# Attention in a four-layer kernel: the spread maximum and the value sums take turns in two PSUM banks

## The chip, the cores and the metric

The kernel runs on one core of a Trainium2 chip. The metric is the device time of one execution in microseconds (us); the figure for a kernel is the median of its timed runs. Engines are named as in the profile: PE (TensorE, matrix products), PEld (its weight loads, which run beside PE), DVE (VectorE), ACT (ScalarE), POOL (GpSimd), SP (SyncE, which issues transfers).

## The reference

Four layers work on `x` of shape (2, 128, 64, 64) in 32-bit floats. Layers 0 and 3 are state-space scans and aren't touched. Layers 1 and 2 are attention over the L = 64·64 = 4096 places of an image, with 128 channels, for each of the two images:

```python
# layer 1 (k and v from an upsampled context; a 3x3 convolution follows)
attn = softmax(einsum('bcn,bcm->bnm', q, k), axis=-1)
out  = einsum('bcm,bnm->bcn', v, attn).reshape(B, C, H, W)
return sr_feat + gamma[0] * conv2d(out, Wp, bp, 1)
# layer 2
attn = softmax(einsum('bci,bcj->bij', q, k), axis=-1)
out  = _conv1x1(einsum('bij,bcj->bci', attn, v), Wo, bo)
return out + x
```

So for each query place n: 4096 scores, their maximum, the exponentials of score minus maximum, their sum, and the sum of values weighted by them.

## The kernel before, in words

**Jobs, groups, units, slots.** Layers 1 and 2 have two images each: four jobs. A job has NG = 16 groups of NQ = 256 queries; there are 64 groups in all. A group goes over the 4096 keys in UPG = 16 units of 256 keys. The order is written out by hand (`tc.manual_schedule()`): one loop over slots, in which every engine gets its instructions in the order of the calls and works through them in that order. A slot issues the score of unit u of one group, the `larger` of the unit before, the softmax steps of the group before it, and two value products; `u` below is slot modulo 16. An odd u or "odd slot" refers to that number.

**The steps of one group, with its first slot called 0.**
- `score(u)`, slots 0 to 15: two products (L961) put the scores of 256 keys by 256 queries into one PSUM bank `s`. ACT copies them to SBUF (`sc`, L966).
- `larger(u)`, one slot later: DVE keeps an elementwise maximum `mx` of 128x2x256 (L973). For u = 0 there is no instruction; for u = 1 both operands are taken at once.
- `turn`, slot 17 (u = 1): PE transposes `mx` in four pieces (L979). `top`, slot 18: DVE reduces them to the maximum `m` of each query (L983), and ACT makes two diagonal matrices `dg` from it (L986). `spread`, slot 19 (u = 3): PE multiplies ones with `dg`, so that bank `pm` holds each query's maximum on all 128 partitions (L992).
- `prob(w)`, w = 0 to 7, slots 21, 23, ..., 35 (odd u): DVE subtracts `pm` from four score tiles in place (L996). `expo(w)` one slot later: ACT (L999). `total(w)` then adds up on POOL (L1004), `total_end` closes it (L1008, L1009).
- `value(u)`, slots 24 to 39: two products (L1016) add onto bank `av`. The group thus has its values for u = 8 to 15 and then 0 to 7 of the slot number.
- `den`, slot 40 (u = 8): PE sums over partitions (L1021), DVE takes the reciprocal (L1023). `finish`, slot 42 (u = 10): DVE multiplies reciprocal and `av` (L1029 or L1036).
- `query`, at u = 10: the next group's queries (L943), with an ACT bias (L945).

Two records on PE stand for each product call in 32-bit floats, one for a transpose. So a score unit or a value unit is four records.

**What is between.** `put` hangs other steps onto slots, after the calls above: key and value pieces of the next job, and after each image of layer 1 the convolution, for groups 1 to 8 of the two jobs that follow: `columns` at u = 10 (four DVE instructions, L1065 to L1068), and `product` at u = 11, 12, 13 and 14 (six PE records each, L1076).

**PSUM.** The eight banks are: `misc` 1, `s` 4 (used in turn by scores, queries, `turn` and `den`), `pm` 1, `av` 2. A bank holds 512 numbers on each partition; `pm` and `av` fill half of one.

Of the kernel before, what the change touches and what calls it, by code (L numbers as in the profile page):

```python
# [8 lines left out]
AF = mybir.ActivationFunctionType  # L9
ALU = mybir.AluOpType  # L10
AX = mybir.AxisListType
PSUM = bass.MemoryType.PSUM

P = 128
# [37 lines left out]
def _bc(ap, axis, shape):  # L52
    return ap.unsqueeze(axis).to_broadcast(shape)
# [3 lines left out]
def conv_seq_kernel(ctx: ExitStack, tc: tile.TileContext, a: dict, out: bass.AP):  # L57
    nc = tc.nc
    mm = nc.tensor.matmul
    act = nc.scalar.activation  # L60
# [3 lines left out]
    def gt(shape, name, pool=None, **kw):  # L64
        return (pool or gp).tile(shape, F32, tag=name, name=name, **kw)
# [14 lines left out]
    ident = cst[:, _CI : _CI + 128]  # L80
    ones = gt([P, P], "ones")
# [16 lines left out]
    with ExitStack() as c0:  # L98
# [153 lines left out]
        def turn(j):  # L252

            nc.scalar.copy(
                xnt[:, 3 + j * T : 3 + (j + 1) * T].rearrange("p (w h) -> p w h", h=H),
                xn[:, 3 : L + 3].rearrange("p (h w) -> p w h", w=W)[:, 8 * j : 8 * j + 8, :],
            )

        class Chunk:
# [110 lines left out]
            def spread(self, what, i):  # L370

                src = (self.ddu if what == "dus" else self.ddt)[i]
                t = wt(what, 2, (P, 4, T))
                for n in range(4):
                    nc.sync.dma_start(t[32 * n : 32 * n + 32], src.rearrange("(k d) t -> d k t", d=32))
                for q in range(2):
                    getattr(self, what)[2 * i + q] = t[:, 2 * q : 2 * q + 2, :]
# [118 lines left out]
        with tc.manual_schedule():  # L496
# [114 lines left out]
            for k, c in enumerate(chunks):  # L611
# [3 lines left out]
                def at(u):  # L615
                    return (c, u) if 0 <= u < 16 else ((old, u + 16) if u < 0 else (new, u - 16))

                A, V, M, G = {}, {}, {}, {}  # L620
                if old is not None:
# [5 lines left out]
                if new is not None:  # L627
# [6 lines left out]
                    M[5], V[6] = lambda: new.pt(1), lambda: new.dt_(1)  # L634
                    G[7], G[8] = lambda: new.dtu_(0), lambda: new.dtu_(1)
                    if not new.rev:
# [23 lines left out]
                if k in turns:  # L660
                    A[11] = (lambda: turn(turns[k]),)

                for s in range(16):
# [7 lines left out]
                    if cp is not None:  # L671
                        cp.s_hc(up)
                    if s in G:
                        G[s]()

# [136 lines left out]
    with ExitStack() as c1:  # L812
        NQ = 256
        NG = L // NQ
        NU = L // 512
        UPG = 2 * NU
# [13 lines left out]
        def bank(tag, shape=(P, T), bufs=1):  # L830
            return ps.tile(list(shape), F32, tag=tag, name=tag, bufs=bufs)
# [4 lines left out]
        def small(tag, shape, bufs=None):  # L836
            return sm.tile(list(shape), F32, tag=tag, name=tag, bufs=bufs)
# [23 lines left out]
        class Job:  # L861
# [77 lines left out]


            def query(self, g):
                pq = bank("s", bufs=4)
                mm(pq[:, :NQ], lhsT=self.wqT, rhs=x[:, self.b, g * NQ : (g + 1) * NQ], start=True, stop=True)  # L943
                q = small("q", (P, NQ))
                act(q, pq[:, :NQ], AF.Identity, bias=self.bq)  # L945
                return q

        class Group:
# [20 lines left out]
            def larger(self, u):  # L969
                if u == 0:  # L970
                    self.mx = small("mx", (P, 2, NQ))
                else:
                    nc.vector.tensor_max(self.mx, self.s[0][:, 0:2, :] if u == 1 else self.mx, self.p[u])  # L973

            def turn(self):
                self.pt = bank("s", (P, 2, 2, P), bufs=4)
                for h in range(2):
                    for o in range(2):
                        nc.tensor.transpose(self.pt[:, h, o, :], self.mx[:, o, h * P : (h + 1) * P], ident)  # L979

            def top(self):
                m = small("m", (P, 2))
                nc.vector.tensor_reduce(m, self.pt, AX.XY, ALU.max)  # L983
                self.dg = small("dg", (P, 2, P))
                for h in range(2):
                    act(self.dg[:, h, :], ident, AF.Copy, scale=m[:, h : h + 1])  # L986

            def spread(self):

                self.pm = bank("pm", (P, NQ))  # L990
                for h in range(2):
                    mm(self.pm[:, h * P : (h + 1) * P], lhsT=ones, rhs=self.dg[:, h, :], start=True, stop=True)  # L992

            def prob(self, w):
                s = self.s[w]
                nc.vector.tensor_sub(s, s, _bc(self.pm[:, :], 1, [P, 4, NQ]))  # L996

            def expo(self, w):
                act(self.s[w], self.s[w], AF.Exp)  # L999
# [9 lines left out]
                self.adds.tensor_add(a_[:, 0, :], a_[:, 0, :], a_[:, 1, :])  # L1009

            def value(self, u):
                if u == 0:
                    self.av = bank("av", (P, NQ), bufs=2)
                for o in range(2):
                    m = 2 * u + o
                    mm(self.av, lhsT=self.job.v[m // 8][:, m % 8, :], rhs=self.s[u // 2][:, m % 4, :],  # L1016
                       start=(m == 0), stop=(m == 31))

            def den(self):
                self.pd = bank("s", (P, NQ), bufs=4)  # L1020
                mm(self.pd, lhsT=ones, rhs=self.sum[:, 0, :], start=True, stop=True)  # L1021
                self.rb = small("rb", (P, NQ))
                nc.vector.reciprocal(self.rb, self.pd)  # L1023
# [82 lines left out]
        def put(slot, *steps):  # L1106
            for i, f in enumerate(steps):
                todo.setdefault(slot + i, []).append(f)

        def piece(slot, j, what, qd, later=0):  # L1110

            steps = []

            def first():
                steps.extend(getattr(j, what)(qd))
                steps[0]()

            n = 2 if j.layer == 2 else 7 if what == "value_piece" else 5
            put(slot, first, *[lambda i=i: steps[i]() for i in range(1, min(n, 5))])
            put(slot + 5 + later, *[lambda i=i: steps[i]() for i in range(5, n)])  # L1120
# [69 lines left out]
        with tc.manual_schedule():  # L1190
            k0, k1 = (jobs[0].key_piece(qd) for qd in range(2))
            k0[0]()
            nc.sync.dma_start(m1[:, 0:128], a["m1"][:, 0:128])
            k1[0]()
            nc.sync.dma_start(m1[:, 128:], a["m1"][:, 128:])
            nc.sync.dma_start(m2, a["m2"])
            for f in k0[1:]:
                f()
            groups[0].q = jobs[0].query(0)
            for f in k1[1:]:  # L1200
                f()
            piece(0, jobs[0], "key_piece", 2)
            piece(4, jobs[0], "key_piece", 3)
            for qd in range(4):
                piece(8 + 5 * qd, jobs[0], "value_piece", qd, 2)
            put(50, second, thirds, second_bias)
            put(60, middle_taps)

            def at(slot):
                n, u = divmod(slot, UPG)  # L1210
                return (groups[n], u) if slot >= 0 and n < len(groups) else (None, 0)

            for slot in range((len(groups) + 2) * UPG):
                u = slot % UPG
                G = at(slot)[0]
                if G is not None:
                    G.score(u)
                    nxt = at(slot + UPG)[0]
                    if u == 10 and nxt is not None:
                        nxt.q = nxt.job.query(nxt.g)  # L1220
                G, d = at(slot - 1)
                if G is not None:
                    G.larger(d)
                G = at(slot - UPG)[0]
                if G is not None:
                    if u == 1:
                        G.turn()
                    if u == 2:
                        G.top()
                    if u == 3:  # L1230
                        G.spread()
                G, d = at(slot - UPG - 5)
                if G is not None and d % 2 == 0:
                    G.prob(d // 2)
                G, d = at(slot - UPG - 6)
                if G is not None and d % 2 == 0:
                    G.expo(d // 2)
                G, d = at(slot - UPG - 8)
                if G is not None:
                    G.value(d)  # L1240
                G, d = at(slot - UPG - 7)
                if G is not None and d % 2 == 0 and d:
                    G.total(d // 2)
                G, d = at(slot - 2 * UPG)
                if G is not None:
                    if d == 6:
                        G.total_end()
                    if d == 8:
                        G.den()
                    if d == 10:  # L1250
                        G.finish()
                for f in todo.get(slot, []):
                    f()
# [4 lines left out]
    with ExitStack() as c3:  # L1258
# [252 lines left out]
        V, G = nc.vector, nc.gpsimd  # L1511
# [263 lines left out]
```

## Time and profile before

| | |
|---|---|
| median of three runs | 6548.74 us (6545.72 to 6561.89) |
| the profiled execution, from its first to its last instruction | 6564.3 us |
| the attention stage in it | about 3470 to 5595 us |
| busy in the whole span | PE 89%, DVE 86%, POOL 83%, ACT 68% |
| one score or value unit on PE, start to start | 0.86 to 0.87 us |
| one `prob` on DVE, mean | 1212 ns |
| one `larger` on DVE, mean | 680 ns |
| one reciprocal on DVE, median | 1757 ns |

The page gives the span of the profiled execution and no time around it. It is 15.6 us, or 0.24%, above the median of the timed runs and 2.4 us above the longest of them. In a line of groups the columns are: line, engine and operation, output and inputs, shapes, count, busy time and mean ns of one, idle time just before and what ended it. In a line of the timeline: start in us, length in us, engine, line, operation, output and inputs; in brackets the idle time before it and what ended it. The length of a PE record ends with its result, later than the start of the next record.

### The profile page before, as it was taken

Reading aid. Unit: us, or ns where it says so; the run is one execution under the profiler, and the core shown is the slowest. Engines: PE = TensorE matmul, PEld = TensorE weight load, DVE = VectorE, ACT = ScalarE, POOL = GpSimd, SP = SyncE. Lnnn points to the kernel's source line nnn. Section 1 sums busy time; section 2 is a strip of 40 time slices with the busy share of each in tenths; the row PEclk is TensorE's granted clock in tenths of the full one; section 3 lists DMA queues with packets and bytes.
Section 4 is the critical chain, followed back from the end, with each engine's and each line's share of the span. In section 5 each row is a group of like instructions: output and inputs, shape, how many; then the busy total and the mean of one; then the engine's idle time right before and its main releaser. Section 6 shows DMA issues by size and latency. Waiting matters only on the chain. (4 is left out here: it accounts for less than half of the span.)

```text
span 6564.3 us, 66618 instructions
## 1 busy us (share of the span) xinstructions
PE 5817.9 (89%) x20014; PEld 2781.5 (42%) x20014; DVE 5628.5 (86%) x4540; ACT 4487.8 (68%) x7771; POOL 5420.7 (83%) x2543
## 2 busy tenths in 40 slices
PE   8888888888888888888888999999999999898888
PEld 2222222222222222222226888888888788222221
DVE  7999999999999999999997766666666766899997
ACT  7887778877788777887766665555556565555453
POOL 6999999999999999999995666655666566788886
PEclk7888777877788777887779999999999999889897
DMA  6566656566666666556650000000000000877775
GB/s 181 145 156 161 161 142 146 146 150 148 152 155 151 153 152 152 146 146 152 151 137 19 2 4 3 1 1 1 1 1 1 2 6 7 205 173 179 181 180 121
DMA packets 400476, 700.36 MB, mean 107 GB/s; under 512 B 74089, under 2 KB 76658, under 8 KB 399730
## 3 DMA queue, kind: packets, MB, share of 16 engines
q1 hardware_dynamic: 399232, 694.33, 43.3%
q8 instruction: 157, 2.57, 0.2%
q14 instruction: 205, 1.68, 0.1%
q10 hardware_dynamic: 882, 1.78, 0.1%
HBM read 584.53 MB, written 111.28 MB: 106 GB/s over the span
## 5 line engine op out<-in xcount | busy, mean ns | idle before, releaser
L383 POOL TENSOR_TENSOR dbu<-dus,bs 128x1024 f32<-128x1024 f32 x1024 | 2448.1, 2440 | 116.9 <-DVE h L427 98.8
L427 DVE TENSOR_TENSOR_SCAN h<-da,hst,dbu 128x1024 f32<-128x1024 f32 x896 | 2090.9, 2340 | 86.1 <-ACT dbu L411 80.7
L396 ACT ACTIVATE da<-dts,aneg 128x512 f32<-128x512 f32 (+1 forms) x2048 | 1410.1, 689 | 357.1 <-DVE h L427 318.9
L1004 POOL TENSOR_TENSOR sum<-sum,sc 128x1024 f32<-128x1024 f32 x378 | 898.1, 2376 | 504.1 <-ACT sc L999 500.4
L966 ACT COPY sc<-s 128x512 f32<-128x512 f32 x1024 | 596.9, 585 | 767.8 <-PE s L961 639.2
L961 PE MATMUL s<-q,k 128*128 128x256 f32 x4096 | 1053.8, 380 | 9.7 <-ACT lo L919 5.5
L1016 PE MATMUL av<-sc,v 128*128 128x256 f32 x4096 | 1051.2, 380 | 9.1 <-ACT sc L999 9.1
L450 PE MATMUL y<-hc,cst 128*32 128x512 f32 x4096 | 880.4, 753 | 200.2 <-DVE hc L439 186.6
L973 DVE TENSOR_TENSOR mx<-mx,s 128x512 f32<-128x512 f32 x896 | 609.3, 680 | 452.5 <-ACT sc L966 449.2
L439 DVE TENSOR_TENSOR hc<-h,pc 128x1024 f32<-128x1024 f32 x704 | 841.9, 1196 | 9.5 <-PE y L450 7.4
L961 PEld LDWEIGHTS s<-q,k 128*128 128x128 f32 x4096 | 777.0, 191 | 126.9 <-issue 8.8
L1016 PEld LDWEIGHTS av<-sc,v 128*128 128x128 f32 x4096 | 768.0, 190 | 112.9 <-ACT sc L999 14.1
L437 POOL TENSOR_TENSOR hc<-h,cs 128x1024 f32<-128x1024 f32 x320 | 770.0, 2406 | 1.2 <-issue 1.2
L416 PE MATMUL pc<-xd,sel 16*128 16x512 f32 x1024 | 707.0, 780 | 0.2
L1407 POOL TENSOR_TENSOR A<-A,D 128x1024 f32<-128x1024 f32 x224 | 526.9, 2370 | 138.8 <-DVE D L1412 102.1
L996 DVE TENSOR_TENSOR sc<-sc,pm 128x1024 f32<-128x1024 f32 x512 | 620.5, 1212 | 0.9 <-PE pm L992 0.9
L999 ACT ACTIVATE sc<-sc 128x1024 f32<-128x1024 f32 x512 | 541.8, 1058 | 41.2 <-DVE sc L996 41.0
L450 PEld LDWEIGHTS y<-hc,cst 128*32 128x32 f32 x4096 | 125.9, 120 | 858.3 <-DVE hc L439 427.6
L340 PE MATMUL misc<-xd,w_dt 9*128 9x512 f32 x504 | 364.6, 810 | 128.1 <-ACT x L479 68.5
L411 ACT ACTIVATE dbu<-hst,dbu,df 128x1 f32<-128x1 f32 x896 | 337.6, 377 | 65.3 <-POOL dbu L383 42.7
L1424 PE MATMUL q<-xs,room 32*128 32x512 f32 x840 | 291.1, 706 | 63.1 <-DVE A L1430 62.1
L416 PEld LDWEIGHTS pc<-xd,sel 16*128 16x128 f32 x1024 | 181.6, 218 | 350.2 <-issue 296.8
(315 smaller groups left out, 7792.9 us busy)
## 6 DMA issues: line engine op xcount, KB each, us to landing
dts<-ddt SPq DMA_DIRECT2D x512, 256.0 KB, 5.4
dus<-ddu SPq DMA_DIRECT2D x512, 256.0 KB, 5.1
D<-rows SPq DMA_DIRECT2D x448, 256.0 KB, 6.0
bs<-rows SPq DMA_DIRECT2D x1024, 64.0 KB, 4.9
cs<-rows SPq DMA_DIRECT2D x1024, 64.0 KB, 3.2
ddt<-dt SPq DMA_DIRECT2D x128, 256.0 KB, 2.0
ddu<-dtu SPq DMA_DIRECT2D x128, 256.0 KB, 4.0
dtr<-ddt SPq DMA_DIRECT2D x448, 64.0 KB, 2.0
```

Source lines behind the costliest of these rows:

```text
L383: nc.gpsimd.tensor_mul(t, self.dus[q], _bc(self.bs[g], 1, [P, 2, T]))
L396: act(t[:, i, sl], self.dts[q][:, i, sl], AF.Exp, scale=an[:, g, 2 * q + i : 2 * q + i + 1])
L416: mm(t, lhsT=sel[32:48, 4 * g : 4 * g + 4, :].rearrange("p n d -> p (n d)"), rhs=self.xd[32:48, :], start=True, stop=True)
L427: nc.vector.tensor_tensor_scan(ho, ai, bi, init, ALU.mult, ALU.add)
L437: nc.gpsimd.tensor_mul(t, self.h[u], _bc(self.cs[gq(u)[0]], 1, [P, 2, T]))
L439: nc.vector.tensor_mul(t, self.h[u], _bc(self.pc[u // 2], 1, [P, 2, T]))
L450: mm(self.y[q // 2][r : r + 32, :], lhsT=sum4, rhs=self.hc[u][:, i, :], start=False, stop=(u % 8 >= 6), skip_group_check=True)
L961: mm(p[:, o, :], lhsT=j.k[m // 8][:, m % 8 * P : m % 8 * P + P], rhs=self.q, start=True, stop=True)
L973: nc.vector.tensor_max(self.mx, self.s[0][:, 0:2, :] if u == 1 else self.mx, self.p[u])
L996: nc.vector.tensor_sub(s, s, _bc(self.pm[:, :], 1, [P, 4, NQ]))
L1004: self.adds.tensor_add(self.sum, self.s[0] if w == 1 else self.sum, self.s[w])
L1016: mm(self.av, lhsT=self.job.v[m // 8][:, m % 8, :], rhs=self.s[u // 2][:, m % 4, :], start=(m == 0), stop=(m == 31))
```

## The change

Three things are different. First, `spread` no longer multiplies ones with a diagonal: it transposes a column of `m`, broadcast to 128 columns, in two pieces; the two ACT instructions for `dg` are gone. Second, DVE joins the two halves of `mx` to one (`join`, called right after the last `larger` of a group), so that `turn` has two transposes in place of four and `top` reduces half as many numbers. Third, the banks: `pm` and `av` of a group are now the halves of one bank `pmav`, of which there are two, taken in turn by the groups; `query`, `turn` and `den` share one bank `aux`; the four `s` banks are left to the scores (and to two late steps of the next layer).

```diff
             def query(self, g):
-                pq = bank("s", bufs=4)
+                pq = bank("aux")
...
+            def join(self):
+                nc.vector.tensor_max(self.mx[:, 0, :], self.mx[:, 0, :], self.mx[:, 1, :])
+
             def turn(self):
-                self.pt = bank("s", (P, 2, 2, P), bufs=4)
+                self.pt = bank("aux", (P, 2, P))
                 for h in range(2):
-                    for o in range(2):
-                        nc.tensor.transpose(self.pt[:, h, o, :], self.mx[:, o, h * P : (h + 1) * P], ident)
+                    nc.tensor.transpose(self.pt[:, h, :], self.mx[:, 0, h * P : (h + 1) * P], ident)
 
             def top(self):
-                m = small("m", (P, 2))
-                nc.vector.tensor_reduce(m, self.pt, AX.XY, ALU.max)
-                self.dg = small("dg", (P, 2, P))
+                self.m = small("m", (P, 2))
+                nc.vector.tensor_reduce(self.m, self.pt, AX.X, ALU.max)
+
+            def spread(self):
+
+                t = bank("pmav", (P, 2, NQ), bufs=2)
+                self.pm, self.av = t[:, 0, :], t[:, 1, :]
                 for h in range(2):
-                    act(self.dg[:, h, :], ident, AF.Copy, scale=m[:, h : h + 1])
-
-            def spread(self):
-
-                self.pm = bank("pm", (P, NQ))
-                for h in range(2):
-                    mm(self.pm[:, h * P : (h + 1) * P], lhsT=ones, rhs=self.dg[:, h, :], start=True, stop=True)
+                    nc.tensor.transpose(self.pm[:, h * P : (h + 1) * P],
+                                        self.m[:, h : h + 1].to_broadcast([P, P]), ident)
 
             def prob(self, w):
                 s = self.s[w]
-                nc.vector.tensor_sub(s, s, _bc(self.pm[:, :], 1, [P, 4, NQ]))
+                nc.vector.tensor_sub(s, s, _bc(self.pm, 1, [P, 4, NQ]))
...
             def value(self, u):
-                if u == 0:
-                    self.av = bank("av", (P, NQ), bufs=2)
...
             def den(self):
-                self.pd = bank("s", (P, NQ), bufs=4)
+                self.pd = bank("aux", (P, NQ))
...
                     G.larger(d)
+                    if d == UPG - 1:
+                        G.join()
```

## The prediction

> **What bounds the kernel now.** I read the page's slices first (the attention stage has PE at nine tenths, DVE and POOL at six), then the groups of the page, the waits of PE in the stage, and one group on the timeline. The groups:
>
> ```profile
> L966 ACT COPY sc<-s 128x512 f32<-128x512 f32 x1024 | 596.9, 585 | 767.8 <-PE s L961 639.2
> L961 PE MATMUL s<-q,k 128*128 128x256 f32 x4096 | 1053.8, 380 | 9.7 <-ACT lo L919 5.5
> L1016 PE MATMUL av<-sc,v 128*128 128x256 f32 x4096 | 1051.2, 380 | 9.1 <-ACT sc L999 9.1
> L973 DVE TENSOR_TENSOR mx<-mx,s 128x512 f32<-128x512 f32 x896 | 609.3, 680 | 452.5 <-ACT sc L966 449.2
> L996 DVE TENSOR_TENSOR sc<-sc,pm 128x1024 f32<-128x1024 f32 x512 | 620.5, 1212 | 0.9 <-PE pm L992 0.9
> ```
>
> Scores and values alone keep PE busy for 2105 of the stage's some 2125 us (3470 to 5595), and PE hardly waits for either. ACT and DVE wait for PE. So PE sets the pace, and whatever makes it wait is paid in full. Its waits between 3500 and 5560 us:
>
> ```profile
> PE pm L992 <- DVE sc L996: 49.8, 52, 1.6
> PE pm L992 <- ACT sc L966: 7.7, 8, 1.1
> ```
>
> That is the one regular wait: the next group's `spread` wants the single `pm` bank while the last `prob` still reads it. On the timeline (group period 30.56 us, from one reciprocal's start, 5338.55, to the next, 5369.11):
>
> ```profile
> 5338.55 1.76 DVE L1023 RECIPROCAL rb<-s 128x256 f32<-128x256 f32 x1 [1.66 <-PE s L1021]
> 5340.22 0.63 DVE L973 TENSOR_TENSOR mx<-mx,s 128x512 f32<-128x512 f32 x1
> 5340.77 1.21 DVE L996 TENSOR_TENSOR sc<-sc,pm 128x1024 f32<-128x1024 f32 x1
> ...
> 5345.69 1.03 PE L961 MATMUL s<-q,k 128*128 128x256 f32 x4
> 5345.70 0.69 DVE L973 TENSOR_TENSOR mx<-mx,s 128x512 f32<-128x512 f32 x1 [0.47 <-ACT sc L966]
> 5346.30 1.21 DVE L996 TENSOR_TENSOR sc<-sc,pm 128x1024 f32<-128x1024 f32 x1
> 5346.55 1.03 PE L1016 MATMUL av<-sc,v 128*128 128x256 f32 x4
> 5346.75 0.59 ACT L966 COPY sc<-s 128x512 f32<-128x512 f32 x1
> 5347.41 1.03 PE L961 MATMUL s<-q,k 128*128 128x256 f32 x4
> ...
> 5357.10 1.21 DVE L996 TENSOR_TENSOR sc<-sc,pm 128x1024 f32<-128x1024 f32 x1
> 5358.46 0.68 PE L992 MATMUL pm<-dg,ones 128*128 128x128 f32 x4 [0.95 <-DVE sc L996]
> ```
>
> Units follow each other every 0.865 us. A value unit (5346.55) runs while DVE subtracts `pm` (5346.30): today they use different banks. And a bank is never used by two engines at once here: the `larger` of most units needs nothing from ACT, yet 449 us of DVE's idle time before L973 end with ACT's copy of the same scores. Two engines that only read one bank are kept apart.
>
> **Bank sharing, the part that decides.** With `pm` and `av` halves of one bank, the same must hold between `prob` on DVE and `value` on PE. The built order of the changed program says so: the values at u = 9, 11, 13, 15, 1 and 3 carry a wait on DVE, and the `prob` ahead of them (the group's third to eighth) comes after PE's values of the slot before, by its own wait or by an earlier one on its engine. At u = 5 and 7 `prob` reads the other bank. Queued behind the waiting value on PE are all later scores, so ACT and DVE starve too.
>
> *The usual odd slot (u = 13, 15).* S is the start of the score in the slot before. Its records end at S+1.03, ACT copies from S+1.08 to 1.67, `larger` starts at 1.70, `prob` 0.60 later (5345.70 to 5346.30) at 2.30, ends at 3.51, and PE starts 0.15 after (5358.31 to 5358.46), at S+3.66. Unhindered the value would start after three units, S+2.595. Stall: 1.07 us. The lower bound is that `larger` is early and only the value before counts (it ends at S+1.90, `prob` from 1.95 to 3.16): 0.72.
>
> *u = 1*: no `larger`, and two transposes (0.22) lie between: 1.95+1.21+0.15 less 2.595 and 0.22, 0.50. *u = 3*: 1.07 less the new `spread` (0.22), 0.85. *u = 11*: the query (0.43) lies between score and value, so `prob` follows the value's end at S+2.38 and PE starts at 3.74, not 3.025: 0.71.
>
> *u = 9*: `den` and the reciprocal come first on DVE. From V, the start of the value at u = 8: `den` is over at V+1.46, the reciprocal starts at 1.50, `larger` 1.67 later, `prob` 0.55 after that (5338.55, 5340.22, 5340.77), PE at V+1.50+1.67+0.55+1.21+0.15 = V+5.08; unhindered at V+2.16. Stall: 2.92 us. Today that delay vanishes in the four score banks.
>
> *Groups with a convolution (16 of 64)*: `columns` at u = 10 takes 1.44+0.86+0.50+0.50 = 3.29 us on DVE, ahead of the `prob` at u = 11. From the value at u = 9: 0.60+0.33+3.29+0.60+1.21 = 6.1 us, against 3.89 unhindered: 2.2. The products at u = 12 and 14 (six records, 1.29) cover the 1.07 at u = 13 and 15.
>
> Sums: 2.92+0.71+2·1.07+0.50+0.85 = 7.12 us in 48 groups, 2.92+2.2+0.50+0.85 = 6.47 in 16: 342+104 = **445 us**. With the lower bounds (0.72 at 13 and 15, 0.50 at 3) it is 6.07 and 6.1, 390. Upwards, a stalled value must also show its first weight load, 0.19 us by its row: 64·6·0.19 = 73 more.
>
> The Trainium skill, "PSUM — Partial Sum Buffer" (section "PSUM bank collisions raise a hardware error"), speaks against this change: it says that two engines collide in a bank even at different addresses, and asks for semaphores by bank. By that rule all six waits are needed; had it been by address, the sum would have only the gains below.
>
> **What the change takes away.** The wait for `pm` goes, 49.8+7.7 and 1.2 for ACT's `dg`: 59 us. `turn` halves (four records in 0.44, start to start, so 0.22), and `spread` falls from four records in 0.52 to two, taken at a transpose's 0.11 each (upper bound: nothing gained if broadcasting costs what is saved): 0.22+0.30 in 64 groups, 33 us. Together **92 us**. The two `dg` (0.69 us of ACT per group), the shorter `top` and the added `join` (nearest row, a 128x256 operation, 0.41 us) cost or bring nothing: DVE idles about 2.1 us before each even-slot `larger` of the new rhythm, and the join stands over 2 us ahead of `turn`. Were that cover gone, the join would cost 64·0.41 = 26. `query` in `aux` waits for the reciprocal, which at u = 9 is over by V+3.3, before the query's turn. No DMA changes.
>
> **The clock.** One long PE gap in the stage, 4011.48 to 4014.23 us (2.75 us, waiting for POOL), is followed by this (the seventh column is the granted clock):
>
> ```profile
> 4012.00:4014.00 2.00, 0.00 (x0) 0.00 (x0) 0.01 (x1) 0.00 (x0) 2.00 (x2) 1.00 0.00 0
> 4014.00:4015.00 1.00, 0.77 (x5) 0.77 (x6) 0.00 (x0) 0.08 (x1) 0.17 (x1) 0.89 0.00 0
> 4015.00:4018.00 3.00, 3.00 (x8) 2.36 (x8) 0.00 (x0) 1.84 (x3) 0.00 (x0) 0.50 0.00 0
> 4018.00:4019.00 1.00, 1.00 (x7) 0.82 (x6) 0.23 (x1) 0.21 (x1) 0.10 (x1) 0.90 0.00 0
> ```
>
> Half clock for 3.4 us, 1.7 us lost. Gaps of 1.69 us (before 5575.65) and 1.43 had no such sequel. The stall at u = 9 is 2.92 less the 0.17 by which a result outlasts its record: a gap of 2.75 too. Bounds: never (0) and in all groups (64·1.7 = 109). The single row of that length lost the clock, the shorter ones didn't; I take 4 in 10, **44 us**. The Trainium skill, "TensorE: Matmul & The Clock Gate" (section "What's actually happening"), wants an idle window of about 3.4 us for the drop; by that the term would be 0, and the row above is against it.
>
> **Sum.** 445 − 92 + 44 = 397 on a span of 6564.3, 6961. The span lies 15.6 over the median of the timed runs: 6945 us.
>
> **Rivals.**
> - *Clock lost in every group* (0.12): all 109 and the weight loads' 73: 445−92+182 = 535, 7084 us. For it the row above; against it 5570 to 5590 us, where PE is busy for 72 and 80% of ten microseconds each at full clock.
> - *Only the reciprocal bites* (0.08): if DVE gets ahead so that the other five `prob`s end before PE is ready: 64·2.92 − 92 = 95, 6644 us. Against it: `prob` alone takes 1.21 us and only one unit of 0.865 lies between the values that bracket it.
> - *Faster* (0.08): the waits fall on values that DVE has long served, and the gains stand: 6549 − 92 = 6457 us, PE almost without a gap. This decides as soon as `prob`, from the preceding value's end to PE's restart (0.05+1.21+0.15), fits into what PE has between; it has 0.865 and needs 1.4. A fourth of this chance is a tie.
> - *My forecast* (0.72), own range 6846 (lower bounds, no clock lost) to 7045.
>
> **Numbers.** The range, 6800 to 7070, takes the forecast's case whole and part of the first rival; the other two and the rest are left out. A measurement of this kernel tells about 0.3% from no change. Faster 0.06, same 0.02, slower 0.92.
>
> **What would show it.** Right: after the change PE has new idle time, ended by DVE's subtraction, before the values (now L1015): some 7 us per group, 384 waits or fewer where products cover them, the longest about 2.9 us at u = 9; DVE's subtraction waits for PE's value; the wait before `spread` is gone; the period of a group without convolution is near 36 to 37 us in place of 30.6. Wrong: values that start every 1.73 us throughout; stalls at u = 9 only; or a granted clock near 0.5 through whole groups, which no term here holds.

## The result, and the profile after

The changed kernel takes 6938.25 us (median of 4 runs, 6935.52 to 6948.86) against 6550.14 us for the kernel before, measured beside it. The ratio is 1.0595 (95% interval 1.058 to 1.061): slower by 6%. The profiled execution spans 6936.3 us, 372 us more than that of before. The attention stage, from the first score's start to the last value's end, grew from 2118.1 to 2510.1 us; the other layers, which the change doesn't touch, happened to be 20 us shorter.

The page's groups after the change, in the same columns as before:

```profile
L1015 PE MATMUL pmav<-sc,v 128*128 128x256 f32 x4096 | 1125.8, 399 | 343.6 <-DVE sc L997 341.6
L966 ACT COPY sc<-s 128x512 f32<-128x512 f32 x1024 | 598.7, 586 | 1187.1 <-PE s L961 1109.8
L961 PE MATMUL s<-q,k 128*128 128x256 f32 x4096 | 1087.4, 390 | 6.8 <-ACT lo L919 5.5
L997 DVE TENSOR_TENSOR sc<-sc,pmav 128x1024 f32<-128x1024 f32 x512 | 621.6, 1214 | 85.7 <-PE pmav L1015 85.4
```

The value products (L1016 before, L1015 now) had 9.1 us of idle time ahead of them and now have 343.6, ended by DVE's subtraction. The subtraction itself takes as long as before (1214 ns), but now waits 85.4 us for PE's values. The scores, products of the same shape (L961), hardly wait (6.8 us). ACT's idle time before its copies has grown by 419 us, and the part of it that PE's scores end by 471: it starves behind PE. So a loop has appeared: DVE waits for a value, the next value waits for DVE. The waits of PE between 3500 and 5940 us, the three most costly of five, show that the former first line, `spread` waiting for `pm`, is gone:

```profile
PE pmav L1015 <- DVE sc L997: 329.1, 333, 4.2
PE misc L896 <- POOL up L936: 2.8, 1, 2.8
PE pmav L1015 <- ACT sc L966: 1.8, 1, 1.8
```

One group on the timeline, without convolution, some of its lines. The first is the restart at u = 9 (one period, 38.0 us, later it comes again in the last line), the second the restart at u = 13, an odd slot of the usual kind, the third and fourth the subtraction and the restart at u = 15:

```profile
5661.17 1.16 PE L1015 MATMUL pmav<-sc,v 128*128 128x256 f32 x4 [2.66 <-DVE sc L997]
...
5672.10 1.13 PE L1015 MATMUL pmav<-sc,v 128*128 128x256 f32 x4 [0.86 <-DVE sc L997]
...
5675.43 1.21 DVE L997 TENSOR_TENSOR sc<-sc,pmav 128x1024 f32<-128x1024 f32 x1
5676.70 1.13 PE L1015 MATMUL pmav<-sc,v 128*128 128x256 f32 x4 [0.88 <-DVE sc L997]
...
5694.19 1.03 PE L1015 MATMUL pmav<-sc,v 128*128 128x256 f32 x4
5695.05 0.59 PE L1020 MATMUL aux<-sum,ones 128*128 128x256 f32 x2
5695.68 1.76 DVE L1022 RECIPROCAL rb<-aux 128x256 f32<-128x256 f32 x1 [1.66 <-PE aux L1020]
5697.90 1.21 DVE L997 TENSOR_TENSOR sc<-sc,pmav 128x1024 f32<-128x1024 f32 x1
5699.16 1.17 PE L1015 MATMUL pmav<-sc,v 128*128 128x256 f32 x3 [2.66 <-DVE sc L997]
```

The subtraction that began at 5675.43 ends at 5676.64; PE restarts at 5676.70. At u = 9 the chain is longer: sum over partitions, reciprocal, `larger`, subtraction, value. The idle time in brackets is counted from the end of PE's last result; measured from one record's start to the next, less the 0.216 us that a record takes, the stall is 2.82 us at u = 9 and 1.02 at u = 13 and 15.

The clock around that first restart (start:end; the seventh column is the granted clock):

```profile
5657.00:5661.00 4.00, 1.51 (x8) 0.98 (x6) 3.31 (x3) 1.57 (x3) 2.35 (x1) 1.00 0.00 0
5661.00:5662.00 1.00, 0.83 (x4) 0.76 (x5) 1.00 (x3) 0.00 (x0) 0.00 (x0) 1.00 0.00 0
5662.00:5665.00 3.00, 3.00 (x9) 2.41 (x8) 0.30 (x2) 0.66 (x2) 0.00 (x0) 0.52 0.00 0
```

Work is there again, but PE runs at half clock for three microseconds. In the trace's clock record the stage has 47 such stretches, 184 us in all; before the change it had one of 3.4 us.

### The profile page after: what moved, and what is told of

The parts are those of the page before. It is cut to its first block, busy times and chain, and to the rows that moved or that the text cites. A ratio compares the mean times of both kernels' runs of the same rounds, so it can differ in the third digit from the quotient of the medians.

```text
span 6936.3 us, 66161 instructions
## 1 busy us (share of the span) xinstructions
PE 5908.6 (85%) x19758; PEld 2791.1 (40%) x19758; DVE 5672.8 (82%) x4604; ACT 4462.3 (64%) x7643; POOL 5410.2 (78%) x2543
## 3 DMA queue, kind: packets, MB, share of 16 engines
q14 instruction: 206, 1.69, 0.1%
## 4 chain that ended last, share of the span: by engine, by line
PE 34%; DVE 17%; POOL 12%; DMA 12%; ACT 11%; issue 10%; SPq 3%; ACTq 0%; POOLq 0%; DVEq 0%
PE pmav L1015 12%; PE s L961 9%; POOL dbu L383 7%; DVE sc L997 6%; DVE h L427 4%; POOL hc L437 3%; DMA dus<-ddu 3%; ACT da L396 3%; PE misc L281 3%; DMA D<-rows 2%; DVE hc L439 2%; DMA cs<-rows 2%; ACT sc L966 2%; DVE D L1413 2%; DMA dts<-ddt 2%
## 5 line engine op out<-in xcount | busy, mean ns | idle before, releaser
L1015 PE MATMUL pmav<-sc,v 128*128 128x256 f32 x4096 | 1125.8, 399 | 343.6 <-DVE sc L997 341.6
L961 PE MATMUL s<-q,k 128*128 128x256 f32 x4096 | 1087.4, 390 | 6.8 <-ACT lo L919 5.5
L1015 PEld LDWEIGHTS pmav<-sc,v 128*128 128x128 f32 x4096 | 774.3, 196 | 560.9 <-DVE sc L997 461.5
L961 PEld LDWEIGHTS s<-q,k 128*128 128x128 f32 x4096 | 801.3, 196 | 133.4 <-issue 9.8
L997 DVE TENSOR_TENSOR sc<-sc,pmav 128x1024 f32<-128x1024 f32 x512 | 621.6, 1214 | 85.7 <-PE pmav L1015 85.4
```

The source lines that it names most:

```text
L961: mm(p[:, o, :], lhsT=j.k[m // 8][:, m % 8 * P : m % 8 * P + P], rhs=self.q, start=True, stop=True)
L997: nc.vector.tensor_sub(s, s, _bc(self.pm, 1, [P, 4, NQ]))
```

## The experiments

The theory: the whole loss comes from `pm` and `av` lying in one bank; the join, the fewer transposes and the broadcast column are a small gain by themselves; and the stall at u = 9 also costs the clock. The rivals: the new operations cost time, or the bank `aux` does; the clock drops for another reason.

**1. The new operations alone** (join, two transposes, broadcast `spread`), with the banks of before:

```diff
-                self.pt = bank("aux", (P, 2, P))
+                self.pt = bank("s", (P, 2, P), bufs=4)
...
-                t = bank("pmav", (P, 2, NQ), bufs=2)
-                self.pm, self.av = t[:, 0, :], t[:, 1, :]
+                self.pm = bank("pm", (P, NQ))
```

The diff is against the changed kernel; `query` and `den` go back to `s`, and `av` to two banks of its own.

> The kernel before with its banks, and only the join, the two transposes and the broadcast spread added. Theory (all the loss is the shared bank): PE sheds four records less per group at turn and spread, 33 us, and the wait for pm at spread stays at about 0.9 us: 6517 us, no wait of a value on DVE, one half-clock interval as before. Rival (join or broadcast column cost time): a value or turn waits for DVE, or the two spread transposes take as long as the four records they replace: 6550 or more.

Measured: 6532.35 us, ratio 0.9953 to before (0.9938 to 0.9969). Its wait of `spread` stands as before:

```profile
PE pm L991 <- DVE sc L996: 52.7, 61, 1.5
PE av L1016 <- ACT sc L999: 9.1, 12, 1.4
...
PE s L981 <- DVE mx L976: 7.3, 6, 2.1
```

So the operations bring about 31 us by the ratio (0.47% of 6556.58, the median of before beside it; the interval is 20 to 41) and 29.6 by the stage (2088.5 us), and none of the loss is theirs. The join is not quite free: `turn` waited for it six times, 7.3 us in all, where before it had waited once, 0.9 us.

**2. The banks alone**, with the diagonal, the four transposes and no join:

```diff
-                self.pm = bank("pm", (P, NQ))
+                t = bank("pmav", (P, 2, NQ), bufs=2)
+                self.pm, self.av = t[:, 0, :], t[:, 1, :]
...
-                pq = bank("s", bufs=4)
+                pq = bank("aux")
```

> The kernel before with only the banks changed: pm and av of a group in one bank, query, turn and den in one. Theory: the waits of values on DVE are there as in the changed kernel. PE has about 0.5 us more work per group at u = 1 and 3, but there DVE sets PE's restart, so that work is covered: about 6940 us, at most 33 more. Rival (the join and the broadcast bring the loss): 6550.

Measured: 6941.32 us, ratio 1.0578 (1.0558 to 1.0598), the same as the changed kernel within the intervals, and a stage of 2509.7 us against 2510.1, with the same kind of wait:

```profile
PE pmav L1015 <- DVE sc L997: 312.5, 278, 4.2
```

The banks are the whole loss. The additional PE work (28 us in the stage, by the pitches of its records) is lost in it, because it lies where DVE sets PE's restart.

**3. Own banks, everything else as changed.** To make room, the scores have three banks in place of four:

```diff
-                t = bank("pmav", (P, 2, NQ), bufs=2)
-                self.pm, self.av = t[:, 0, :], t[:, 1, :]
+                self.pm = bank("pm", (P, NQ))[:, :]
...
+                if u == 0:
+                    self.av = bank("av", (P, NQ), bufs=2)
```

> The changed kernel with pm and av in banks of their own again (one for pm, two for av, and therefore three score banks instead of four); join, broadcast spread and the shared aux bank stay. Theory (the loss is the sharing of pm and av): no value waits for DVE any more, the wait of spread for pm is back with about 0.9 us per group, no clock drops: about 6525 us, and up to some 40 more if three score banks don't cover the reciprocal. Rival (aux or the added join and transposes bring part of the loss): 6600 or more with values waiting for DVE.

Measured: 6528.96 us, ratio 0.9944 (0.9924 to 0.9964), as experiment 1. The stage takes 2088.6 us, 0.1 more than in experiment 1. No value waits for DVE, the old wait of `spread` is back, and one half-clock stretch is left:

```profile
PE pm L991 <- DVE sc L996: 52.7, 61, 1.5
PE s L961 <- DVE mx L973: 8.7, 9, 2.4
...
PE aux L981 <- DVE mx L976: 5.5, 6, 1.9
```

The second and third lines are what the three score banks (2.5 us in experiment 1) and the join cost; `aux` adds nothing that shows. So the loss goes with `pm` and `av` in one bank. They also are one tile there (`pmav`); no run puts two tiles into one bank, so whether the program's waits go by bank or by tile stays open.

**4. Useless work in the gap.** Ahead of the value at u = 9 PE gets three products more:

```diff
                 if G is not None:
+                    if d == 1:
+                        f = misc()
+                        for i in range(3):
+                            mm(f[:, 0:NQ], lhsT=ones, rhs=x[:, 0, 0:NQ], start=True, stop=True)
                     G.value(d)
```

> The changed kernel with six PE records of useless work (1.3 us) ahead of the value at u = 9, where PE waits for the reciprocal and the subtraction. Theory (the gap of 2.7 us costs the clock): the start of the value stays, the gap halves, the half-clock intervals go from 47 to under 10, and with more work on PE the kernel is faster by up to 46 x 1.7 = 78 us: 6860 to 6880. Rival (the clock drops for another reason, or does not matter): 6938. Second rival (the work is on the path): 64 x 1.3 = 83 us slower, 7021.

Measured: 6876.41 us, ratio 1.0478 to before (1.046 to 1.0496), against 1.0595 (1.058 to 1.061) without the filling. More work on the busiest engine made the kernel some 77 us faster by the ratios (62 by the medians, which come from different sessions); the stage is 76 us shorter (2434.0 us). One restart at u = 9, and then two stretches of 40 us, each longer than a group:

```profile
5646.09 1.13 PE L1015 MATMUL pmav<-sc,v 128*128 128x256 f32 x4 [1.36 <-DVE sc L997]
```

```profile
5634.00:5674.00 40.00, 35.52 (x161) 29.53 (x160) 24.95 (x30) 19.82 (x29) 20.71 (x11) 1.00 0.00 1
5674.00:5714.00 40.00, 35.51 (x161) 29.52 (x160) 24.95 (x30) 19.82 (x29) 22.03 (x13) 1.00 0.00 1
```

The gap is 1.36 us in place of 2.66, the clock stays at 1.00, and three half-clock stretches (10 us) are left of 47. None of the three came after a gap of 1.36 us: they follow gaps of 2.07, 2.67 and, waiting for POOL, 2.77 us. So the long gap is what cost the clock.

**5. Without the reciprocal.** A copy stands in its place, so this kernel leaves out the division:

```diff
-                nc.vector.reciprocal(self.rb, self.pd)
+                nc.vector.tensor_copy(self.rb, self.pd)
```

> The changed kernel with DVE's reciprocal (1.76 us) replaced by a plain copy of the sums, so that the division is left out. Theory (the reciprocal ahead of the subtraction makes the stall at u = 9 long): the stall falls from 2.8 to 1.5 us, 64 x 1.3 = 85 us, and the gap no longer costs the clock, 46 x 1.7 = 78 us: about 6775 us. Rival (the stall at u = 9 has another cause, the division is covered): 6938. Between them, if the clock still drops: 6855.

Measured: 6804.79 us, ratio 1.0361 (1.0337 to 1.0385). Against the changed kernel's 1.0595 that is 0.0234, some 153 us of 6550, where 163 had been expected; the stage is 151 us shorter (2358.8 us). The copy took 0.425 us; the stall at u = 9 is 1.54 us (2.82 with the reciprocal), and four half-clock stretches are left, each after a gap of 2.59 us or more. The reciprocal ahead of the subtraction makes the long stall.

**6. A version that beats both:** experiment 1 with `spread` one slot later, so that the next group's maximum is spread after the last subtraction that reads `pm`, and PE has a value and a score in between.

```diff
-                    if u == 3:
+                    if u == 4:
                         G.spread()
```

> The kernel before with its banks, the join, the two transposes and the broadcast spread as in e1_work_only, and spread called one slot later (u = 4), behind the last subtraction that reads pm. Theory: the wait for pm (59 us) is covered by the value and the score between, on top of the 33 us: 6458 us. Rival (the first subtraction at u = 5 now comes too late and the exponentials delay the values): 6517 or more, with values waiting for ACT.

Measured: 6464.5 us, ratio 0.9855 (0.9838 to 0.9872) to before, and a stage of 2023.1 us, 95 less than before. The wait for `pm` isn't in its list of PE's waits any more; the longest item there is now

```profile
PE av L1016 <- ACT sc L999: 9.1, 12, 1.4
```

and from 5330 to 5391 us, about two groups, PE is busy all the time:

```profile
5330.00:5391.00 61.00, 61.00 (x288) 53.62 (x287) 46.61 (x58) 37.30 (x55) 40.84 (x21) 1.00 0.00 1
```

One `pm` bank is enough here when nobody asks for it too early.

## Why the prediction was right, point by point

The forecast was 6945 us, the measurement 6938.25; the sum was +397, and the stage grew by 392 us. The agreement is better than the terms, and that much of it is luck. So is the step from the span to the median: I took 15.6 us off a span of 6961, while the span of after is 6936.3 and lies 2 us under the median; what is outside the stage took 4446 us in the profile of before, 4426 in that of after, and 4438 to 4451 in those of the six experiments. The terms below are worked out from the start times of PE's records within the stage, before and after: what is over the usual distance to the next record goes to the stall, the wait or the clock.

| term, us | predicted | profiled runs |
|---|---|---|
| PE stalls ahead of values | +445 | +386 |
| work taken from PE, and the wait for `pm` | −92 | −102 |
| half clock | +44 | +84 |
| a restarted value shows its first weight load | 0 (bound 73) | +25 |
| sum | +397 | +393 (the stage: +392) |

**Bank sharing.** Right in its mechanism (experiments 2 and 3) and in its places: stalls at u = 9, 11, 13, 15, 1 and 3, none at u = 5 and 7. At u = 13 and 15 it was 1.02 us (predicted 1.07), at u = 11 0.68 (0.71), at u = 9 2.82 (2.92), at u = 1 0.40 (0.50), at u = 3 0.80 (0.85). Each forecast is a little too long: I took 0.15 us from the subtraction's end to PE's restart, from a product that waited for two engines; a value that waits for DVE restarts after 0.06. Where the error is less than these 0.09, something else was longer than in my sum: at u = 13 ACT's copy starts at S+1.12, not 1.08. There were 342 waits of PE for DVE's subtraction, within the 384 that I had named as the most.

**The convolution's columns**, the mis-sized term: I predicted 2.2 us at u = 11 in 16 groups, and it was 0.68 as elsewhere. (The sum there, 6.1 us, is 6.03; that is 1 us in all.) The four instructions took 1.44, 0.86, 0.50 and 0.50 us in the mean before; after the change all four take 0.48. I carried over durations that belonged to the old rhythm. There POOL was at work beside every one of them that took over 0.6 us, though also beside many that took 0.5; after the change POOL stands idle beside all four in all 16 groups, and DVE is back in time.

**The cover of the products** at u = 12 and 14 held: in groups with a convolution the stall at u = 13 and 15 is zero.

**What is taken away.** Experiment 1 measured 31 us for the operations (predicted 33), experiment 6 some 95 with the wait (1.45% of 6556.58; 92 by the medians; predicted 92). That the join would bring or cost nothing was a little too good, as experiment 1 shows.

**The clock.** Bounds were never and always; I took 4 in 10 groups, and it was 47 of 64. This error and the two above offset each other.

What decides is not the length of the gap alone, and the clock record of the traces shows it. In each of the eight profiles all changes of the clock lie on one grid of 3.413 us, to within 1 ns. In the attention stages of all eight, a stretch of this grid at full clock in which PE idled 2.0 us or more, by its records, was followed by half clock in the next stretch (106 cases); where it idled less, full clock stayed (5070 cases; the two meet at 2.00 us). So a gap of 2.66 us costs the clock or not as it falls on the grid. In the changed kernel 58 restarts at u = 9 have that gap: 44 were followed by half clock; at the other 14 a grid line divides the gap, with no more than 2.0 us on either side. First the stretches about the restart at 5661.17, then another restart with its stretches:

```profile
5658.73:5662.14 3.41, 0.97 (x5) 0.87 (x6) 3.31 (x5) 0.40 (x1) 1.69 (x1) 1.00 0.00 0
5662.14:5665.55 3.41, 3.41 (x10) 2.66 (x9) 0.69 (x1) 1.21 (x3) 0.00 (x0) 0.50 0.00 0
```

```profile
5546.86 1.13 PE L1015 MATMUL pmav<-sc,v 128*128 128x256 f32 x4 [2.65 <-DVE sc L997]
```

```profile
5542.67:5546.09 3.42, 1.54 (x8) 1.00 (x6) 2.71 (x3) 2.14 (x4) 1.79 (x1) 1.00 0.01 2
5546.09:5549.50 3.41, 2.64 (x12) 2.36 (x13) 1.65 (x3) 0.55 (x2) 0.56 (x1) 1.00 0.00 0
```

PE was busy for 0.97 us of the first stretch, idle for 2.44, and the clock dropped; in the second case it was idle for 1.88 us, and the clock stayed. The one row of before, a gap of 2.75 us that lay whole in one stretch, could not tell this, and the gaps of 1.69 and 1.43 us were by themselves too short for it.

**The rivals.** The clock in every group: in 47 of 64, and without the weight loads' full price (its bound of 73 us has six restarts in all groups; with four in those with a convolution it is 67). Only the reciprocal: experiment 5 took its part away and most of the loss stayed. Faster: what PE has between is 0.865 us against 1.21 for the subtraction alone; the gains without the stalls are what experiments 1 and 6 measured. The upper end of my own range, 7045, is stated without a sum. The second sign I had named, a period of 36 to 37 us, holds for groups that kept the clock (36.28 in three without any other work between); with the clock lost it is 37.97.

## What to carry to other kernels

Two tensors of one stage that live in halves of one PSUM bank can be tied to each other, as here by the waits that the program carries: PE adds to one while DVE still reads the other, and each reader's turn was a stop of the matrix engine, 0.4 to 2.8 us, though they share no data. Count what falls between two accesses of the bank, not the banks that are saved, and look first whether a later call ends the old wait. And where PE has to wait anyhow, the length of the gap can matter beyond the gap itself: here each half-clock stretch of 3.4 us lost some 1.7.

## What the runs showed of the hardware

- A PE gap of 2.66 us was followed by half clock in 44 of 58 cases, for 3.4 us or more; a gap of 1.36 us in none of 58 (experiment 4). What separates them in the attention stages of all eight profiles is 2.0 us of idling within one stretch of a grid of 3.413 us. This holds for the stage alone: in the scan layers of before, where PE's products are of other shapes, some of the 148 drops follow a stretch without any idle time in PE's records. The Trainium skill, "TensorE: Matmul & The Clock Gate" (section "What's actually happening"), speaks of an idle window of about 3.4 us; the drop came here after shorter gaps.
- The join, 128x256 numbers with both operands in SBUF, took 1.25 us in the median (0.70 to 1.55), longer than the 0.68 us of a `larger` of 128x512 with an operand in PSUM. POOL's sums ran beside it in all 64 cases; in the changed kernel a single wait, of 0.3 us, was put down to it. The Trainium skill, "SBUF — State Buffer" (section "Who interferes with whom"), says that a DVE instruction with two SBUF inputs contends with a GpSimd one that reads SBUF; join and columns agree with it, but no run here sets it apart from other causes.
- A value that restarts after a wait takes 0.967 us to the next score's start in place of 0.863; I read the 0.10 us as a weight load that nothing hides.
